# Centring the output projection's weights of two Mamba blocks, so that the normalisation behind it needs no mean

## The chip, the cores and the metric

The kernel runs on one core of a Trainium2 chip. Its engines are TensorE (PE, with its weight loads shown apart as PEld), VectorE (DVE), ScalarE (ACT), GpSimd (POOL) and SyncE (SP, which here issues DMAs). The metric is the device time of one execution in microseconds (us), the median over several executions. The profile is of one execution.

## The reference

A 2 x 256 x 32 x 32 image goes through four layers; the change touches the first one only. It is a GroupNorm and two Mamba blocks, each followed by a layer norm over the 256 channels that is added to the block's input:

```python
def layernorm(x, w, b):
    mu = jnp.mean(x, axis=-1, keepdims=True)
    var = jnp.mean(jnp.square(x - mu), axis=-1, keepdims=True)
    return (x - mu) * jax.lax.rsqrt(var + LN_EPS) * w + b
# mamba_block, per token: project 256 -> 2 x 512, convolve over 4 tokens, silu -> xs
h = dA_t * h + dBu_t                  # 512 channels x 16 states, one step per token
y = einsum(h, C_t) + xs * Dp
y = y * silu(res)
out = y @ out_w + out_b               # 512 -> 256
# the layer
xt = xt + layernorm(mamba_block(xt, m1...), ln1_w, ln1_b)
xt = flip(xt)
xt = xt + layernorm(mamba_block(xt, m2...), ln2_w, ln2_b)
```

The mean that the layer norm takes away is the mean over the 256 outputs of `y @ out_w + out_b`. It is linear in `out_w` and `out_b`: if each of the 512 rows of `out_w`, and `out_b`, has its own mean over the 256 columns taken away, the output has mean zero.

## The kernel before, in words

Layer 0 takes the first 1050 us or so. The 2048 tokens (two images of 1024) are kept as 256 channels on two sets of 128 partitions. Each block handles them in four chunks of 512, so there are eight units, 0 to 7: units 0 to 3 are block m1's, 4 to 7 block m2's. At the heart of a unit is `scan` (L525): 16 states, for each of them four quarters of 128 channels, 64 slots in all. For a state POOL multiplies two products of 128 x 1024 (`m_h`, by way of the helper `lined` at L179, which keeps POOL's work in the order written; residual adds, sums and some DMAs go through the same line). For a slot ACT computes a decay `m_da` of 128 x 512 by Exp (L617) into one of three PSUM buffers, and DVE runs the recurrence over 512 tokens in place on `m_h` (L621). The `m_h` tiles have six buffers, two to a state. PE then transposes each finished `m_h` (L575, L577) into one of three PSUM buffers, and its product with C is added up over the states by DVE (L591) or, for some states, put aside by ACT (L589, `m_ya` and `m_s`) and added by a DMA that POOL issues.

Beside the scan of a unit run the front of the next unit (`front`, L411: convolution on PE, whose result ACT takes out of PSUM at L436 as `m_xs`, then Silu under another table of functions, then the step sizes) and the back of the unit before it (`back`, L650). `back` computes the gate (L655), joins the sums, multiplies by the gate (L689), then projects to 256 outputs per token: for each 128 tokens a product of a row of ones with the bias `out_b` (L696) and four products with the 512 x 256 weights `out_sb` (L700). `norm_rows` (L181) normalises the four tiles of 128 x 256 in the chunk. DVE takes each tile's mean and variance (L188, L189); ACT computes the reciprocal root by Ln and Exp (L159, L160); DVE forms an offset, minus the mean times the root, in two small operations of 128 x 4 (L192, L200); and ACT scales and shifts each tile (L202). PE transposes the result, ACT applies the layer norm's own weight and bias (L724), and POOL adds it to the residual `x`. For the last unit of m2 the same is written into another tile.

`load_rest` (L360) loads the gate's weights and the output weights (L369, a DMA of 512 KB from SP): before the first unit for m1, and at slots 37 and 62 of unit 4 for m2, into the same buffer that m1's held. The two bias rows come in one DMA at the start (L101). At the start, `enter` for unit 0 runs alone: PE projects, ACT takes each of four tiles out (`m_pre`, L405), and the first front follows.

The order is made in two steps. For each unit, `layer0` collects a list `steps` of generators, each with a count, a first and an end slot, and a pacing function advances them between the slots of the scan. That is the order in which instructions are written. A scheduler then orders each engine's instructions by when it reckons their operands to be ready, except where an order is forced (`issue_after`, which `lined` and the table loads use). Each engine then executes in the order so found, and an instruction that waits holds up those behind it on its engine.

Of the kernel before, what the change touches and what calls it, by code (L numbers as in the profile page):

```python
# [10 lines left out]
F32 = mybir.dt.float32  # L11
I32 = mybir.dt.int32
BF16 = mybir.dt.bfloat16
AF = mybir.ActivationFunctionType
# [5 lines left out]
P = 128  # L20
# [4 lines left out]
C = 256  # L25
# [6 lines left out]
NDC = DI // P  # L32
# [37 lines left out]
class Net:  # L70
# [110 lines left out]
    def norm_rows(self, outs, ins, by=None):  # L181


        nc, n = self.nc, len(ins)
        mv = self.small.tile([P, n, 2], F32, tag="ln_mv", name="ln_mv")
        for i, a in enumerate(ins):
            st = self.small.tile([P, 6], F32, tag="ln_st", name="ln_st")
            nc.vector.bn_stats(out=st, in_=a)  # L188
            nc.vector.bn_aggr(out=mv[:, i, :], in_=st)  # L189
        if by is nc.scalar:  # L190
            off = self.small.tile([P, n], F32, tag="ln_off", name="ln_off")
            nc.vector.tensor_sub(off, self.zeros[:, :n], mv[:, :, 0])  # L192
        rs = self.small.tile([P, n], F32, tag="ln_rs", name="ln_rs")
        if by is nc.gpsimd:
            nc.gpsimd.tensor_scalar_add(rs, mv[:, :, 1], self.eps5)
            nc.gpsimd.tensor_tensor(rs, rs, self.power[:, :n], ALU.pow)
        else:
            self.rstd(rs, mv[:, :, 1])
        if by is nc.scalar:
            nc.vector.tensor_mul(off, off, rs)  # L200
            for i, (o, a) in enumerate(zip(outs, ins)):
                nc.scalar.activation(  # L202
                    o, a, AF.Identity, scale=rs[:, i : i + 1], bias=off[:, i : i + 1]
                )
            return
        for i, (o, a) in enumerate(zip(outs, ins)):
            nc.vector.tensor_scalar(o, a, mv[:, i, 0:1], rs[:, i : i + 1], ALU.subtract, ALU.mult)
# [79 lines left out]
class Mamba:  # L287
# [73 lines left out]
    def load_rest(self):  # L361

        net, nc, m, wpool = self.net, self.net.nc, self.m, self.wpool
        in_w, out_w, xproj_w, dt_w = self.weights
        self.gate_sb = wpool.tile([P, NCC, DI], F32, tag="gate_w", name=f"{m}_gate_sb")
        nc.sync.dma_start(self.gate_sb, in_w[:, :, DI:])
        yield
        self.out_sb = wpool.tile([P, NDC, C], F32, tag="out_w", name=f"{m}_out_sb")
        nc.sync.dma_start(self.out_sb, out_w)  # L369

        if self.kept:
            nc.sync.dma_start(self.skip_tile(), self.kept[1])
        else:
            self.scaled(self.skip_tile(), f"{m}_D")
        yield

    @staticmethod
    def first(j):
# [364 lines left out]
def paced(n, parts):  # L743

    taken = [0] * len(parts)
    for slot in range(n):
        for i, (steps, many, first, end) in enumerate(parts):
            while taken[i] < many and slot >= first + (end - first) * taken[i] / many:
                next(steps, None)
                taken[i] += 1  # L750
        yield
    for steps, *_ in parts:
        for _ in steps:
            pass
# [11 lines left out]
def layer0(net, x, x_dram, m1, m2, load_image, taps, conv_dram, lg):  # L766
# [4 lines left out]
    tc, nc = net.tc, net.nc  # L771
    with (
# [45 lines left out]
        for u, (m, j) in enumerate(units):  # L818
            joined = u + 1 < len(units)
            ready = done  # L820
            if joined:
                done = [islice(b, 2 * NDC + 11) for b in done]
            steps = [(b, NDC, 4, 20) for b in done]
            if u:
                m.due.update(units[u - 1][0].due)
            fronts = []
            for a, k in units[u + 1 : u + 2]:
                if k == 0:
                    a.load()
                fronts.append(a.front(k))  # L830
                if u == 0:
                    steps.append((a.enter(k), Mamba.ENTER, 0, 10))
            enters = []
            for a, k in units[u + 2 : u + 3]:
                if k == 0:
                    a.load_in()
                enters.append(a.enter(k))
            steps += [(f, Mamba.HEAD - 3, 0 if u else 10, 25) for f in fronts]
            steps += [(b, NDC + (not joined), 25 if joined else 19, 37 if joined else 35) for b in done]
            steps += [(f, 3, 25, 33) for f in fronts]  # L840
            if u == NCH - 2:

                steps.append((blocks[1].fetch_diagonals(), 1, 34, 35))
            rest = m.load_rest() if u and j == 0 else iter(())
            steps += [(rest, 1, 37, 38)]
            for n, first, end in Mamba.STEPS:
                steps += [(f, n, first, end) for f in fronts]
            steps += [(b, 8, 45, 53) for b in done]
            steps += [(e, Mamba.ENTER - 1, 36, 44) for e in enters]
            steps += [(e, 1, 59, 60) for e in enters]  # L850
            steps += [(b, 2, 1, 5) for b in late]
            steps += [(b, 1, 54, 55) for b in done] + [(b, 2, 56, 58) for b in done]
            if u + 1 == len(units):
                steps += [(b, 2, 60, 63) for b in done]
            late = ready
            steps += [(rest, 1, 62, 63)]
            if u + 1 < len(units):
                more = not u
                for n, first, end in ((2, 12, 32), (4, 35, 47), (3, 58, 63)):
                    steps += [(islice(aside, n + more), n + more, first, end)]  # L860
            else:
                last.close()
                m.ps_da = last.enter_context(tc.tile_pool(name="m_da2", bufs=2, space=PSUM))
                ps_acc = last.enter_context(tc.tile_pool(name="m_acc", bufs=1, space=PSUM))

                def place(u):
                    pool, tag, w = {
                        3: (one, "pre", TC + 3), 0: (two, "xs", TC), 1: (two, "delta", TC),
                        2: (two, "du", TC),
                    }[u]  # L870
                    a = pool.tile(
                        [P, NDC, w], F32, tag=tag, name=f"early_{u}",
                        bufs=3 if tag == "xs" else None,
                    )
                    return taps.load(u, a.rearrange("p d t -> p (d t)"))

                pair = {u: place(u) for u in taps.ORDER}
                def early():
                    for k in range(2):
                        a = ps_acc.tile([P, TC], F32, tag="acc", name=f"early_acc{k}")  # L880
                        acc = {k: taps.bank(a)}
                        yield from taps.convolve(0, pair, acc)
                        taps.read(acc, lg)

                steps += [(early(), 112, 3, 63)]
            own = m.back(j, u + 1 == len(units), u + 2 < len(units))
            if u + 1 == len(units):

                steps += [(islice(own, 5), 5, 44, 58)]
            before = m.scan(j, before, paced(63, steps), u == 0, u + 1 == len(units))  # L890
            done = [own]
# [1249 lines left out]
def conv_attn_hybrid(ctx: ExitStack, tc: tile.TileContext, a: dict, out: bass.AP):  # L2141
# [9 lines left out]
    with tc.tile_pool(name="conv_w", bufs=2) as convw:  # L2151
        def load_x(b):
            for cc in range(NCC):
                nc.sync.dma_start(x[:, cc, b, :], a["x"][b, cc])

        load_x(0)
        taps = Taps(net, convw, main, x, a["l1_w1"], a["l1_w2"])
        layer0(
            net, x, a["x"],
            [a[f"m1_{k}"] for k in ("in_w", "out_w", "xproj_w", "dt_w")],  # L2160
            [a[f"m2_{k}"] for k in ("in_w", "out_w", "xproj_w", "dt_w")],
            lambda: load_x(1), taps, conv_dram, lg,
        )
# [144 lines left out]
```

## Time and profile before

| | |
|---|---|
| median of 6 runs | 2037.71 us (2033.49 to 2049.37) |
| the profiled execution | 2038.84 us, of which the span is 2037.1 us |
| granted PE clock, mean over the span | 0.966 |
| PE, busy | 1865.2 us, 92% of the span |
| PE weight loads, busy | 1339.8 us, 66% |
| DVE, busy | 1334.9 us, 66% |
| POOL, busy | 1071.2 us, 53% |
| ACT, busy | 946.5 us, 46% |
| ACT's scaling pass L202 in layer 0 | 28 + 4 passes, 13.5 + 1.9 us |
| DVE's statistics L188 in layer 0 | 32 passes, 12.3 us |

In a line of instructions the fields are: the start (or, in groups, none), the busy time in us, the engine, the line of the kernel, the operation, output<-inputs by the program's names, shapes and the number of instructions; in square brackets, or after the last bar, the idle time of the engine just before and the instruction that ended it. In groups "12.3, 420" is the busy time of the group in us and the mean duration of one in ns. Where an engine works through a pipeline, successive instructions overlap a little, so the busy time of a group can be smaller than the count times the mean.

### The profile page before, as it was taken

How to read it: one execution, taken by the hardware profiler on the slowest of the kernel's cores; microseconds unless marked ns; L12 is line 12 of the kernel's file. 1: busy time of each engine (PE TensorE's matmuls, PEld its weight loads, DVE VectorE, ACT ScalarE, POOL GpSimd, SP SyncE). 2: the span in 40 equal slices, each digit the busy share in tenths (PEclk: the TensorE clock that was granted, in tenths of full speed). 3: DMA queues.
4: the chain of work that ended last, by engine and by line, in shares of the span. 5: the costliest groups of instructions: out<-in, count | busy, mean ns of one | idle time of the engine just before them, and what ended most of it. 6: DMA issues, size and time to landing. Idle time of an engine off the chain costs nothing. (4 is left out here: it accounts for less than half of the span.)

```text
span 2037.1 us, 27880 instructions
## 1 busy us (share of the span) xinstructions
PE 1865.2 (92%) x9938; PEld 1339.8 (66%) x9938; DVE 1334.9 (66%) x2141; ACT 946.5 (46%) x1713; POOL 1071.2 (53%) x726
## 2 busy tenths in 40 slices
PE   8788988898898988899999989999999899999995
PEld 3465665656565665655666555568999656799994
DVE  6989998999889989897614285774222455652223
ACT  4787777777877767764302253332111122221111
POOL 7888896978979798985404250012333200023330
PEclk9889999999999999899999999999999999999997
DMA  4334354343535334362130100146999400358995
GB/s 151 98 91 120 88 145 112 88 110 85 143 91 134 77 86 112 88 156 47 32 57 1 52 0 1 37 183 250 328 328 335 162 21 21 143 191 319 328 329 196
DMA packets 98856, 271.77 MB, mean 133 GB/s; under 512 B 35915, under 2 KB 54224, under 8 KB 82324
## 3 DMA queue, kind: packets, MB, share of 16 engines
q1 hardware_dynamic: 81268, 198.03, 28.9%
q0 software_dynamic: 14432, 68.31, 13.5%
q10 hardware_dynamic: 3008, 3.55, 0.5%
q8 instruction: 83, 1.36, 0.3%
q14 instruction: 65, 0.53, 0.1%
HBM read 200.80 MB, written 22.77 MB: 110 GB/s over the span
## 5 line engine op out<-in xcount | busy, mean ns | idle before, releaser
L179 POOL TENSOR_TENSOR m_h<-m_du,m_b 128x1024 f32<-128x1024 f32 x254 | 603.8, 2463 | 143.0 <-PE m_ht L577 61.3
L617 ACT ACTIVATE m_da<-m_delta,m_aneg 128x512 f32<-128x512 f32 x512 | 349.4, 694 | 150.7 <-DVE m_h L621 145.2
L621 DVE TENSOR_TENSOR_SCAN m_h<-m_da,m_state,m_h 128x512 f32<-128x512 f32 x256 | 314.3, 1268 | 20.6 <-POOL m_h L179 13.1
L577 PEld LDWEIGHTS m_ht<-ident,m_h 128*128 128x128 f32 x1600 | 193.4, 146 | 191.9 <-DVE m_h L621 64.8
L621 DVE TENSOR_TENSOR_SCAN m_h<-m_da,m_h 128x512 f32<-128x512 f32 x256 | 299.6, 1210 | 18.9 <-ACT m_da L617 13.3
L577 PE MATMUL m_ht<-ident,m_h 128*128 128x128 f32 x1600 | 253.6, 286 | 59.0 <-DVE m_h L621 29.7
L591 DVE SCALAR_TENSOR_TENSOR m_ya<-m_ht,m_ct,m_ya 128x512 f32<-128x512 f32 x324 | 232.6, 737 | 59.9 <-PE m_ht L577 50.9
L2067 PEld LDWEIGHTS h<-xts,we_l_late 128*128 128x128 f32 x2048 | 238.4, 192 | 7.7 <-issue 2.8
L2067 PE MATMUL h<-xts,we_l_late 128*128 128x128 f32 x2048 | 239.7, 275 | 3.3 <-DMA we_l_late<-in_l_experts_dram 1.5
L2075 DVE TENSOR_TENSOR hid<-hid,h 128x512 f32<-128x512 f32 x79 | 54.3, 687 | 232.2 <-PE h L2067 231.8
L1806 POOL DMA_INDIRECT x_l_early<-l_zs,l_source x15 | 17.3, 1156 | 341.6 <-ACT pt L1570 139.5
L2074 ACT ACTIVATE hid<-h 128x512 f32<-128x512 f32 x79 | 47.2, 597 | 314.3 <-PE h L2067 314.3
L575 PE MATMUL m_ht<-ident,m_h 128*128 128x128 f32 x896 | 138.2, 302 | 29.9 <-ACT m_s L589 11.9
L575 PEld LDWEIGHTS m_ht<-ident,m_h 128*128 128x128 f32 x896 | 122.0, 208 | 52.8 <-DVE m_h L621 19.9
L1806 POOL DMA_INDIRECT x_l_late<-l_zd,source x64 | 65.4, 1022 | 147.9 <-PE xt L2050 143.8
L2082 PE MATMUL o<-we_l_late,hid 128*128 128x256 f32 x512 | 122.7, 381 | 4.1 <-DVE y L2087 2.8
L2089 POOL DMA_INDIRECT l_yd<-y,target x64 | 65.4, 1022 | 104.1 <-DVE y L2087 92.0
L430 PE MATMUL m_conv<-m_pre,m_taps 128*128 128x512 f32 x240 | 116.9, 605 | 3.4 <-ACT m_xs L436 3.3
L589 ACT ACTIVATE m_s<-m_ht,m_ct 128x512 f32<-128x512 f32 x156 | 104.5, 687 | 29.6 <-DMA m_yb<-m_s 12.9
L2082 PEld LDWEIGHTS o<-we_l_late,hid 128*128 128x128 f32 x512 | 91.8, 190 | 15.3 <-DVE y L2087 3.9
L1001 PE MATMUL early_acc<-x,early 128*98 128x448 f32 (+24 forms) x308 | 100.3, 452 | 0.4 <-DVE lg L1018 0.4
L1001 PE MATMUL acc<-x,pair 128*98 128x416 f32 (+21 forms) x308 | 93.3, 450 | 0.0
(412 smaller groups left out, 3119.7 us busy)
## 6 DMA issues: line engine op xcount, KB each, us to landing
we_l_late<-in_l_experts_dram SPq DMA_DIRECT2D x64, 1536.0 KB, 9.1
m_yb<-m_s POOLq DMA_DIRECT2D x39, 1024.0 KB, 8.6
m_b<-m_bd SPq DMA_DIRECT2D x128, 256.0 KB, 3.5
we_l_early<-in_l_experts_dram SPq DMA_DIRECT2D x15, 1536.0 KB, 8.1
m_ya<-m_yb POOLq DMA_DIRECT2D x7, 1024.0 KB, 8.8
w<-in_l_w_dram SPq DMA_DIRECT2D x21, 256.0 KB, 6.5
l_yl<-l_yd SPq DMA_DIRECT2D x8, 512.0 KB, 11.1
l_zd<-l_z SPq DMA_DIRECT2D x7, 512.0 KB, 3.0
```

Of the source, the lines that this page charges most:

```text
L179: self.line = do(*args, **named)
L430: nc.tensor.matmul(ps, lhsT=self.taps[:, dc * 4 + k, :], rhs=pre[:, dc, k : k + TC], start=(k == 0), stop=(k == 3),)
L575: nc.tensor.matmul(a, lhsT=h, rhs=net.ident, start=True, stop=True)
L577: nc.tensor.transpose(a, h, net.ident)
L589: nc.scalar.activation(to[:, i, :], ps, AF.Copy, scale=c)
L591: nc.vector.scalar_tensor_tensor(ya[:, i, :], ps, c, ya[:, i, :], ALU.mult, ALU.add)
L617: net.decayed = nc.scalar.activation(da, delta[:, dc, :], AF.Exp, scale=self.aneg[:, i : i + 1])
L621: nc.vector.tensor_tensor_scan(h, da, h, 0.0 if first else state[:, n, dc : dc + 1], ALU.mult, ALU.add)
L1001: nc.tensor.matmul(a[:, lo - 16 * k : hi - 16 * k, co : co + n], lhsT=lhsT, rhs=self.x[:, kc, b, lo - r0 : hi - r0, ci : ci + n], start=(u ...
L1806: nc.gpsimd.indirect_dma_start(out=x, out_offset=None, in_=rows[:, :], in_offset=bass.IndirectOffsetOnAxis(ap=source[:, g : g + 1], axis=0 ...
L2067: nc.tensor.matmul(ps[:, at], lhsT=w12[:, s, kc, at], rhs=xt[:, kc * P : (kc + 1) * P], start=(kc == 0), stop=(kc == NCC - 1),)
L2082: gate.o = nc.tensor.matmul(ps[:, :C], lhsT=ht[:, mc * P : (mc + 1) * P], rhs=w[:, 8 + mc, :], start=(mc == 0), stop=(mc == NHC - 1),)
```

## The change

Once per block, `centre` takes the mean over the columns out of each row of the output weights, and out of the bias. It does it in place with ACT: for each of the four tiles of 128 x 256 and for the bias row, a Copy that also adds up its row (`accum_out`); two small passes that turn sums into minus means; and for each tile and the bias an Identity with that number as its bias. That is 12 instructions a block. They are written for slots 6 to 36 of each block's second unit (`j == 1`), ahead of the first `back` of the block. In `norm_rows`, the two small DVE operations on the offset are gone, and ACT's pass is a Copy with a scale alone, without an offset. The statistics are taken as before; of them, only the variance is used where ACT does the pass.

```diff
         for i, a in enumerate(ins):
             st = self.small.tile([P, 6], F32, tag="ln_st", name="ln_st")
             nc.vector.bn_stats(out=st, in_=a)
             nc.vector.bn_aggr(out=mv[:, i, :], in_=st)
-        if by is nc.scalar:
-            off = self.small.tile([P, n], F32, tag="ln_off", name="ln_off")
-            nc.vector.tensor_sub(off, self.zeros[:, :n], mv[:, :, 0])
         rs = self.small.tile([P, n], F32, tag="ln_rs", name="ln_rs")
...
         if by is nc.scalar:
-            nc.vector.tensor_mul(off, off, rs)
             for i, (o, a) in enumerate(zip(outs, ins)):
-                nc.scalar.activation(
-                    o, a, AF.Identity, scale=rs[:, i : i + 1], bias=off[:, i : i + 1]
-                )
+                nc.scalar.activation(o, a, AF.Copy, scale=rs[:, i : i + 1])
             return
...
+    def centre(self):
+
+        nc, w = self.net.nc, self.out_sb
+        sums = self.wpool.tile([P, NDC + 1], F32, tag="centre", name=f"{self.m}_centre", bufs=1)
+        parts = [(w[:, dc, :], sums[:, dc : dc + 1]) for dc in range(NDC)]
+        parts.append((self.out_b, sums[:1, NDC:]))
+        for a, s in parts:
+            nc.scalar.activation(a, a, AF.Copy, accum_out=s)
+            yield
+        nc.scalar.activation(sums[:, :NDC], sums[:, :NDC], AF.Copy, scale=-1.0 / C)
+        nc.scalar.activation(sums[:1, NDC:], sums[:1, NDC:], AF.Copy, scale=-1.0 / C)
+        for a, s in parts:
+            nc.scalar.activation(a, a, AF.Identity, bias=s)
+            yield
...
             rest = m.load_rest() if u and j == 0 else iter(())
             steps += [(rest, 1, 37, 38)]
+            if j == 1:
+                steps.append((m.centre(), 10, 6, 36))
             for n, first, end in Mamba.STEPS:
```

`NDC` is 4 and `C` is 256.

## The prediction

> **What bounds the kernel now.** I read the stretches of the span first, then the idle time of VectorE (DVE) and ScalarE (ACT) by releaser, then the groups of instructions that the change touches, then the timeline around a block's normalisation. The change lies in layer 0 alone (0 to about 1050 us; eight units of 512 tokens, a scan of 115.6 to 121.8 us each and 139.1 for the last). Busy time by stretch (length, PE, weight loads, DVE, ACT, POOL, clock, DMA share, GB/s), alternately from state 12 of a unit to state 5 of the next, and from there to state 12:
>
> ```profile
> 238.00:305.00 67.00, 59.84 (x315) 42.29 (x316) 62.54 (x71) 52.98 (x96) 66.41 (x33) 0.97 0.44 118
> 305.00:357.00 52.00, 44.88 (x225) 28.38 (x223) 44.18 (x49) 38.74 (x65) 33.64 (x18) 0.93 0.41 110
> 357.00:424.00 67.00, 58.95 (x312) 40.27 (x313) 62.46 (x72) 53.24 (x98) 66.76 (x33) 1.00 0.43 111
> ...
> 592.00:658.00 66.00, 56.96 (x303) 39.18 (x303) 62.85 (x69) 51.78 (x97) 65.76 (x33) 1.00 0.46 117
> ...
> 910.00:1045.00 135.00, 131.69 (x623) 83.55 (x621) 83.75 (x124) 44.33 (x69) 54.11 (x38) 0.99 0.18 41
> ```
>
> In the 67 us stretches POOL is busy 99% and DVE 62.5 us, so DVE has 4.5 us of room; the 52 us stretches have no full engine, there chains of DVE, PE and ACT set the length. The last unit is PE's. Who waits for whom (total us, times, longest):
>
> ```profile
> ACT m_da L617 <- DVE m_h L621: 145.2, 188, 6.8
> ...
> DVE m_ya L591 <- PE m_ht L577: 50.9, 43, 5.0
> ...
> DVE m_h L621 <- ACT m_da L617: 20.5, 24, 3.6
> ...
> DVE m_h L621 <- POOL m_h L179: 17.3, 17, 6.4
> ```
>
> ACT mostly waits for DVE's scans to free one of three decay buffers, so it is at most three scans ahead: an ACT instruction that stalls longer than that lead stops the scan.
>
> **What is removed.** The groups of the edit (busy us, mean ns, idle before and its releaser):
>
> ```profile
> L200 DVE TENSOR_TENSOR ln_off<-ln_off,ln_rs 128x4 f32<-128x4 f32 x8 | 7.2, 896 | 4.3 <-ACT ln_rs L160 4.2
> ...
> L192 DVE TENSOR_TENSOR ln_off<-zeros,ln_mv 128x4 f32<-128x4 f32 x8 | 3.6, 450 | 0.0
> ```
>
> These 16 instructions go: 7.2 + 3.6 + 4.3 = 15.1 us at most; measured as the delay of the next DVE instruction at each block (2.3, 1.0, 2.3, 0.9, 2.3, 2.8, 1.0, 0.4) it is 13.0. The first five (8.8 us) lie inside the stretches where POOL is full. A scan that starts earlier there only waits longer for POOL's product, as these two of DVE already do:
>
> ```profile
> 406.42 5.06 DVE L621 TENSOR_TENSOR_SCAN m_h<-m_da,m_state,m_h 128x512 f32<-128x512 f32 x4 [0.38 <-POOL m_h L179]
> 411.95 3.63 DVE L621 TENSOR_TENSOR_SCAN m_h<-m_da,m_state,m_h 128x512 f32<-128x512 f32 x3 [0.47 <-POOL m_h L179]
> ```
>
>  I count these five as nothing; if POOL's limit did not cover them, they would be worth all of it. The sixth (853 us) lies where POOL runs 8 to 10 us ahead; half of 2.8, **-1.3**. The last two lie in PE's unit, 131.69 busy of 135: **-0.4** of 1.4. ACT's 32 scaling passes drop one pointer operand; by rows of 128x512 with two operands (775 ns) and one (687) that is 32 x 0.09 = 2.8 us of an engine with 14 us free in each stretch: 0, at most -2.8.
>
> **What is added, at the start.** The 24 ACT instructions of `centre` are written for states 1 to 8 of each block's second unit, but in the built kernel's order the first block's stand at the very head of ACT: four sums over the output weights come before the first `m_pre`, and the rest between the four `m_pre`.
>
> ```profile
> 6.42 0.34 SPq L369 DMA_DIRECT2D m_out_sb<-in_m_out_w_dram  x1
> ...
> 13.73 0.69 ACT L405 ACTIVATE m_pre<-m_in,cols_sb 128x512 f32<-128x512 f32 x1 [2.70 <-PE m_in L399]
> 15.45 0.69 ACT L405 ACTIVATE m_pre<-m_in,cols_sb 128x512 f32<-128x512 f32 x1 [1.03 <-PE m_in L399]
> ```
>
> The weights take 7.1 us, so they land at 13.5. A sum over 128x256 is in no row; bounds are 373 ns (copies of that shape, L1100) and 565 (L202, two operands). Four take 1.5 to 2.3, so the first `m_pre` starts at 15.0 to 15.8 instead of 13.73, with the projection's third product, which needs its buffer, behind it. Between the others ACT idles 1.03 us, into which two or three of the remaining passes fit each time. What waits is the first convolution, which ends PE's opening at 26.4: **+1.0** (0 if the slack takes it, 2 if the sums are slow).
>
> **What is moved.** POOL's order is unchanged; PE and DVE follow. ACT's order changes in every block's normalisation and the unit after it. At state 1 of the next unit it was (m_xs is line 436, waiting for POOL's residual add):
>
> ```profile
> 401.89 0.69 ACT L617 ACTIVATE m_da<-m_delta,m_aneg 128x512 f32<-128x512 f32 x1 [0.58 <-DVE m_h L621]
> 404.11 0.69 ACT L436 ACTIVATE m_xs<-m_conv,cols_sb 128x512 f32<-128x512 f32 x1 [1.53 <-POOL x L179]
> 404.70 0.68 ACT L589 ACTIVATE m_ya<-m_ht,m_ct 128x512 f32<-128x512 f32 x1
> ```
>
> Now `m_xs` and the second `m_ya` stand ahead of that last decay of state 1. POOL's add is not earlier, so the decay starts at 404.11 + 2 x 0.6 = 405.3, plus the first `m_ya` if it too is queued behind, 405.9: its scan at 406.6 instead of 404.8, +1.8. Behind it the scans of states 2 to 4 catch up what they waited for POOL (0.4 to 0.5), leaving +1.3; DVE at state 5 then does two `m_ya` before the scan that frees ACT for its block of Silus and table loads. I carry **+1.5** into the next stretch for each of three boundaries (units 1-2, 2-3, 3-4): +4.5. Ends for each: 0, if DVE's 4.5 us of room takes it, and 3.0, if the Silu block slips by DVE's two passes (2 x 0.74) as well. Earlier, around states 14 and 15, the scaling and transposed passes also come ahead of two decays; with a scan waiting 1 us longer there, the same room absorbs it before the later stall, so it isn't added.
>
> Between units 4 and 5 the second block's centring comes in. Its first sum stands behind `m_s` of state 13 and waits for its weights, issued at 612.28 with 5.4 us to land: 617.7, where ACT is free at 616.65. That is 1.0 us, plus 0.4 of work, and behind it queue the second `m_s`, the `ln_rs` and the last decay of state 14. Three more sums stand before state 1's decays, and `m_xs` now ahead of the third decay: +1.5 as above and +1.0 of the wait, **+2.5** (1 to 5). The five subtracting passes (0.5 each, by four L202 in 1.93 us) are spread through states 1 to 5 where ACT idles for DVE: 0; without that cover, 2.5, which is in the upper end. Units 5-6 have `m_xs` ahead of two decays: **+1.5** (0 to 3). Unit 0-1 keeps its order: 0. SyncE's only move, one scan row past one or two loads in five units, has rows prefetched four deep: 0, up to 0.5 each. The table loads stay at 24.
>
> **The sum.** +1.0 + 4.5 + 2.5 + 1.5 - 1.3 - 0.4 = +7.8 us on the profiled execution's 2038.84 (span 2037.1): 2046.6. That execution stands 1.1 above the median of 2037.71, so 2045.5 by the median; I say 2046. Within 0.5% (10.2 us) is about what a measurement of this kernel can tell from no change; its six runs spread over 15.9.
>
> **Two rules.** DVE's 16 removed passes took 99 to 2370 ns against 150 when undisturbed, while POOL's products keep 2.35 us around them. The Trainium skill ("SBUF — State Buffer", section "SBUF: two separate sides") says that a VectorE operation with two SBUF inputs and a GpSimd operation share a port pair as an exclusive lock; by that POOL's full stretches could gain up to 16 x 0.15 = 2.4 us, an estimate, and the sum would be +5.4; no row here shows POOL held. DVE's scaling passes of 128x512 took 578 ns (L282), ACT's 687 (L589). The skill ("ScalarE: Activation LUTs", "Rules for kernel authors") gives add and multiply to VectorE rather than ScalarE, which speaks against centring on ACT: 16 passes of half that width, about 0.9 us of ACT by those two rows.
>
> **Rivals.**
> *The removed chain counts in full.* For: its longest pass, up to 2.4 us, holds DVE just where ACT waits for DVE. Against: POOL's 99%. Then 13.0 + 2.8 come off and only +1.0 and +2.5 stay: -12.3, 2026.5 less 1.1, **2025**.
> *The order of ACT costs double.* One place decides: state 1's last decay behind `m_xs`. If the lateness reaches the Silu block whole, each of five boundaries costs 3.0, with the start at 2.0 and the wait for weights 2.0: +19, **2057**. It decides from about 2.2 us a boundary on. For: no decay can be issued until those passes are through, and no scan without it; against: DVE's room.
> *Room takes everything.* DVE's 4.5 us per POOL stretch swallow the stalls: +1.0 + 1.0 - 1.7 = +0.3, less 1.1: **2038**.
>
> **How the numbers follow.** Forecast 0.42 (its own range 2040 to 2052; 0.28 within 0.5%, that is to 2047.9, and 0.14 above); double 0.28; room 0.12; full gain 0.18. So faster 0.18, within 0.40, slower 0.42. Each outer case leaves about half or a third of itself out (0.18/2, 0.28/3), 0.18 in all: 2026 to 2058.
>
> **What would show it.** After: the first `m_pre` at 15 or later; the decay of state 1 behind `m_xs` with its wait for POOL about as long as before; DVE's scan there waiting for ACT; POOL's stretches still 99%. If DVE's waits for POOL shrink while units don't grow, the room was larger; if units 1 to 3 are shorter than 116, POOL was no limit and I am wrong on the side of the gain.

## The result and the profile after

The changed kernel takes 2048.05 us (median of 22 runs, 2043.67 to 2057.21) against 2039.47 us for the kernel before, run beside it (48 runs, 2032.37 to 2049.37). The ratio is 1.0042, with a 95% interval of 1.0031 to 1.0053: it is slower by 8.6 us, or 0.42%. The forecast was +7.8 us on the profiled execution, and 2046 us in all. The profiled execution of the changed kernel took 2051.44 us, its span 2049.7.

Busy time by stretch in the changed kernel, the stretches set to its own units (same columns as before). The first, third and fourth rows are the stretches in which POOL was full:

```profile
241.00:308.00 67.00, 59.66 (x317) 42.60 (x317) 61.08 (x69) 51.90 (x94) 66.42 (x33) 0.97 0.45 118
308.00:361.00 53.00, 45.65 (x238) 29.86 (x237) 47.27 (x52) 41.50 (x73) 36.29 (x19) 0.97 0.42 110
361.00:426.00 65.00, 57.68 (x301) 39.28 (x300) 58.58 (x66) 50.08 (x92) 64.17 (x32) 0.97 0.44 114
...
595.00:661.00 66.00, 58.28 (x294) 40.07 (x292) 56.71 (x64) 51.64 (x101) 63.51 (x32) 0.95 0.44 112
...
914.00:1049.00 135.00, 131.24 (x633) 84.27 (x631) 83.98 (x121) 44.77 (x72) 56.16 (x42) 1.00 0.19 43
```

POOL still has 99% of the stretch around 241 to 308, but 96% of the one around 595 to 661, where the second block's centring falls: there POOL is no longer the full engine. The last unit is PE's as before.

Who waits for whom in layer 0 of the changed kernel (total us, times, longest):

```profile
ACT m_da L626 <- DVE m_h L630: 149.7, 200, 5.1
...
DVE m_ya L600 <- PE m_ht L586: 52.2, 44, 4.7
...
DVE m_h L630 <- ACT m_da L626: 32.0, 35, 3.6
...
ACT m_xs L445 <- POOL x L179: 14.7, 5, 5.8
...
DVE m_h L630 <- POOL m_h L179: 12.9, 8, 6.4
```

In the kernel before, ACT's wait for the add was:

```profile
ACT m_xs L436 <- POOL x L179: 8.6, 5, 4.2
```

The other lines of before stand in the prediction. DVE's scans waited 20.5 us for ACT's decays and now wait 32.0; they waited 17.3 us for POOL's products and now wait 12.9. ACT waited 8.6 us for POOL's residual add before it could take `m_xs` out, now 14.7. DVE's own work fell by 9.3 us over the whole span (1334.9 to 1325.6), and none of it shows in the time.

The place that the prediction replayed, state 1 of unit 3, on ACT and then on DVE:

```profile
401.59 0.69 ACT L626 ACTIVATE m_da<-m_delta,m_aneg 128x512 f32<-128x512 f32 x1 [1.14 <-DVE m_h L630]
405.68 0.69 ACT L445 ACTIVATE m_xs<-m_conv,cols_sb 128x512 f32<-128x512 f32 x1 [3.40 <-POOL x L179]
406.27 1.26 ACT L598 ACTIVATE m_ya<-m_ht,m_ct 128x512 f32<-128x512 f32 x2
407.41 0.70 ACT L626 ACTIVATE m_da<-m_delta,m_aneg 128x512 f32<-128x512 f32 x1
```

```profile
408.14 1.28 DVE L630 TENSOR_TENSOR_SCAN m_h<-m_da,m_state,m_h 128x512 f32<-128x512 f32 x1 [1.69 <-ACT m_da L626]
409.98 7.16 DVE L630 TENSOR_TENSOR_SCAN m_h<-m_da,m_state,m_h 128x512 f32<-128x512 f32 x6 [0.55 <-ACT m_da L626]
```

ACT stands idle for 3.4 us at `m_xs` because POOL's add is no earlier than it was, both `m_ya` go first, and the decay that the scan needs starts at 407.41. In this execution the unit began 1.6 us later than before (395.4 against 393.9). The scan that started at 404.8 before starts at 408.14, so 1.8 us of it is new, as the prediction had it. DVE then waits for ACT where it waited for POOL before.

**A table of stages.** Layer 0 can be split at the starts of DVE's scans: the first scan; then, added up over the eight units, states 0 to 6, states 7 to 12 and states 13 to 15. Each row is one profiled execution; the runs e1 to l4 are described below. Times are in us.

| execution | first scan | states 0-6 | states 7-12 | states 13-15 | last scan ends |
|---|---|---|---|---|---|
| before | 44.1 | 385.1 | 381.4 | 196.7 | 1007.3 |
| before, again (e8) | 44.1 | 385.1 | 382.3 | 197.2 | 1008.8 |
| before, layer 0 alone (l1) | 45.9 | 384.9 | 378.1 | 195.8 | 1004.8 |
| before, new addresses (e2) | 45.1 | 385.0 | 382.4 | 197.2 | 1009.7 |
| changed | 45.6 | 393.8 | 374.8 | 195.9 | 1010.2 |
| changed, layer 0 alone (l2) | 45.2 | 393.1 | 379.3 | 196.5 | 1014.0 |
| changed, old addresses (e1) | 45.5 | 389.1 | 376.6 | 198.9 | 1010.1 |
| normalisation alone (e3) | 45.3 | 391.9 | 382.1 | 198.1 | 1017.3 |
| centring alone (e4) | 45.2 | 386.2 | 382.8 | 198.5 | 1012.6 |
| centring late (e5) | 44.1 | 395.1 | 374.3 | 195.2 | 1008.7 |
| centring late, layer 0 alone (l3) | 43.9 | 397.1 | 381.7 | 193.7 | 1016.4 |
| decays first (e6) | 44.1 | 390.1 | 378.0 | 192.3 | 1004.5 |
| decays first, layer 0 alone (l4) | 45.4 | 391.6 | 375.2 | 193.6 | 1005.8 |
| before, one slot later (e7) | 45.4 | 387.5 | 378.6 | 198.2 | 1009.7 |

In four executions with the order of before, states 0 to 6 take 384.9 to 385.1 us. In the three with the changed order (changed, l2, e1) they take 389.1, 393.1 and 393.8: all are longer, but by 4 to 9 us, so the column tells the two orders apart and doesn't give the price of the change to the microsecond. The same holds for e5 and l3 and for e6 and l4, two executions each of one order in layer 0: 2.0 and 1.5 us apart. Units 3 and 4 do repeat: in the changed order their states 0 to 6 are 1.1 and 2.0 to 2.1 us longer in all three, in e3, e5 and l3 too. Units 5 and 6 do not, and there PE's granted clock differs as well. States 1 and 2 of unit 5 took 12.9 us in the changed kernel at a clock of 0.87, and 10.6 in l2 and e1 at 1.00. Over states 0 to 6 of unit 6 the clock was 0.93 and 0.94 in the changed kernel and l2, and 0.97 in e1 and before. Whether the changed order brings these dips on is open.

States 7 to 12 differ by 4 us between executions of the order of before, so one profile can't tell anything of that size there. The changed kernel's own profile had 374.8 us there and ended layer 0 only 2.9 us late, although 8.8 us had been lost in states 0 to 6. From the first scan to the end of the last, the four executions of before take 958.8 to 964.7 us and the three of the changed order 964.6, 964.6 and 968.8: on the mean 3 us more.

### The profile page after: what moved, and what is told of

Its sections match the earlier page's. It is cut to its first block, busy times and chain, and to the rows that moved or that the text cites. A ratio compares the mean times of both kernels' runs of the same rounds, so it can differ in the third digit from the quotient of the medians.

```text
span 2049.7 us, 27896 instructions
## 1 busy us (share of the span) xinstructions
PE 1868.3 (91%) x9938; PEld 1342.3 (65%) x9938; DVE 1325.6 (65%) x2125; ACT 952.3 (46%) x1747; POOL 1071.0 (52%) x726
## 3 DMA queue, kind: packets, MB, share of 16 engines
q0 software_dynamic: 14432, 68.31, 13.5%
## 5 line engine op out<-in xcount | busy, mean ns | idle before, releaser
L630 DVE TENSOR_TENSOR_SCAN m_h<-m_da,m_state,m_h 128x512 f32<-128x512 f32 x256 | 314.3, 1268 | 23.2 <-POOL m_h L179 12.1
L2078 PE MATMUL h<-xts,we_l_late 128*128 128x128 f32 x2048 | 244.1, 278 | 7.2 <-DMA we_l_late<-in_l_experts_dram 3.7
L2078 PEld LDWEIGHTS h<-xts,we_l_late 128*128 128x128 f32 x2048 | 242.5, 195 | 12.2 <-issue 7.4
L584 PEld LDWEIGHTS m_ht<-ident,m_h 128*128 128x128 f32 x896 | 120.8, 206 | 48.1 <-ACT m_s L598 14.7
```

The lines of the kernel that those rows point to most:

```text
L584: nc.tensor.matmul(a, lhsT=h, rhs=net.ident, start=True, stop=True)
L630: nc.vector.tensor_tensor_scan(h, da, h, 0.0 if first else state[:, n, dc : dc + 1], ALU.mult, ALU.add)
L2078: nc.tensor.matmul(ps[:, at], lhsT=w12[:, s, kc, at], rhs=xt[:, kc * P : (kc + 1) * P], start=(kc == 0), stop=(kc == NCC - 1),)
```

## The experiments

The comparisons below are of the whole kernel unless layer 0 is named, each with the ratio to the kernel before on the same chip.

**e1 and e2: is it the addresses?** The dropped offsets freed 128 bytes per partition in a pool that lies under most tiles, and the sums took 32 back, so most tiles moved by 128 or 96 bytes. e1 is the changed kernel with the sums in the room of the offsets, e2 the kernel before with the offsets in the room of the sums:

```diff
# e1, on the changed kernel
-        sums = self.wpool.tile([P, NDC + 1], F32, tag="centre", name=..., bufs=1)
+        sums = self.net.small.tile([P, NDC + 1], F32, tag="ln_off", name=...)
# e2, on the kernel before (net.offs is the pool m_w)
-            off = self.small.tile([P, n], F32, tag="ln_off", name="ln_off")
+            off = self.offs.tile([P, n], F32, tag="centre", name="ln_off", bufs=1)
```

> The changed kernel with its order of instructions, but the column sums take the room of the dropped offsets, so that every other tile lies at the address it had before the change (in the changed kernel most tiles lie 128 or 96 bytes lower). The profile of the change shows layer 0 ending only 2.9 us later than before, while the medians differ by 8.6. Address theory: the other 5.7 come from the lower addresses; then this run is about +3 us over the kernel before (2042 to 2043) and layer 0 ends +3. Order theory: addresses are nothing, the whole +8.6 stays (2048), and the profiled executions merely differ in the later layers.

> The kernel before, with its order of instructions, but its tiles at the addresses of the changed kernel: the offsets are kept in a tile of 32 bytes where the sums would be. Address theory: +5 to +6 us, nearly all in the later layers. Order theory: no change, within 2 us, layer 0 ending within 0.5 us of before.

e1 measured 1.0021 (1.0006 to 1.0037), 2045.48 us; e2 1.0023 (1.0006 to 1.0040), 2045.95 us. Taken alone they look like an effect of the addresses of 0.2%, about 4 us. Both lie nearer to what the address theory expected (about +3, and +5 to +6) than to the order theory's +8.6 and 0, and the two together (0.21% and 0.23%) make up the changed kernel's 0.42%. The profiles fit that in part: from the end of the last scan to the end of the span, the two executions at the new addresses (changed, e2) took 1039.5 and 1038.8 us, and the eight whole-kernel ones at the old addresses 1029.3 to 1037.0. Against it stands e3 (below), which loses 8.8 us at the old addresses. In layer 0, e2's states 0 to 6 and 13 to 15 are those of before to 0.5 us, so what the addresses cost would arise elsewhere. In e1, states 0 to 6 cost 4.0 us, less than in the changed kernel. Whether the addresses cost nothing or up to about half of the 8.6 us is open.

**e3 and e4: which half of the change costs?** e3 has only the changed normalisation, e4 only the centring in front of the old one; both with tiles at the addresses of before.

```diff
# e3, on the changed kernel: no centring; ACT's Ln writes to the room of the offsets
-            if j == 1:
-                steps.append((m.centre(), 10, 6, 36))
# e4, on the kernel before: centre() added, norm_rows untouched
+            if j == 1:
+                steps.append((m.centre(), 10, 6, 36))
```

> The changed normalisation alone (no offsets, one operand less in ACT's pass), on weights that are not centred, with no centring instructions; tiles at the addresses of before. It leaves out the centring, so the mean is not removed from the output. ACT's and DVE's order is that of the changed kernel in all but the centring's own instructions, so this carries the moved m_xs at state 1. Order theory: layer 0 pays at the boundaries but not at the start: units 3, 4, 5, 6 each show their state 1 longer by 1 to 2 us, layer 0 ends 0 to +3, total 0 to +6. Rival (the removed chain counts in full): -10 to -12 us. Rival (room takes everything): 0 within 1.

> The centring alone, in front of the normalisation as it was before (offsets kept); tiles at the addresses of before; ACT's order is that of before apart from the centring's instructions. Order theory: +1.5 us at the start, where the profile of the change shows the first scan at 45.6 instead of 44.1, and +1 to +2 between units 4 and 5 from the wait for the weights: +2.5 to +3.5 in layer 0 and in total. If the centring carries the whole loss: +8.

e3 measured 1.0043 (1.0024 to 1.0062), 2048.74 us; e4 1.0005 (0.9984 to 1.0026), 2043.38 us against 2042.34. So taking sixteen instructions off DVE costs as much by itself as the whole change, more than expected, and adding 24 to ACT costs little, less than expected in the total. In the table e3 pays 6.9 us in states 0 to 6. Its first scan is late without any centring, as in other runs that have none (last section). e4 pays 1.1 to 1.2 in states 0 to 6, of which 1.1 lie in state 6 of unit 0, ahead of every boundary, where the granted clock was 0.87 over 13.5 us and 1.00 in the kernel before. The expected +1 to +2 between units 4 and 5 shows as 0.4, in unit 5. The order of e3's instructions on ACT is the changed kernel's but for some in units 4 and 5, that of e4 is that of before but for a few in unit 5. The rival in which the removed chain counts in full wanted -10 to -12 for e3: it falls.

The start in the kernel before, and in e4, whose granted clock was 1.00 there as well (PE: start, busy; in brackets the idle time and its releaser):

```profile
11.71 7.13 PE L399 MATMUL m_in<-x,m_in_sb 128*128 128x512 f32 x16 [0.44 <-DVE x L282]
```

```profile
11.82 3.70 PE L414 MATMUL m_in<-x,m_in_sb 128*128 128x512 f32 x8 [0.44 <-DVE x L282]
15.98 3.70 PE L414 MATMUL m_in<-x,m_in_sb 128*128 128x512 f32 x8 [0.46 <-ACT m_pre L420]
```

PE's projection, one unbroken row of 7.13 us before, now breaks after its second product and waits for `m_pre`, as the prediction said. The first scan is 1.1 us later in e4, 1.4 in e1; the prediction had 1.0.

**e5: the centring held back.** Each of its instructions may follow only the decay written just before it, so that the start is as it was, and the second block's sums come after the weights have landed.

```diff
# on e1
+            with tc.issue_after(net.decayed.ins):
                 nc.scalar.activation(a, a, AF.Copy, accum_out=s)
...
+            with tc.issue_after(net.decayed.ins):
                 nc.scalar.activation(a, a, AF.Identity, bias=s)
```

> Both parts of the change, tiles at the addresses of before, but each instruction of the centring may only follow the decay written just before it. So ACT issues none at the start, and the second block's sums come in states 1 to 4 of unit 5, long after its weights have landed. The rest of the order stays that of the changed kernel. Order theory: against the run with both parts at the old addresses (+4.3 us) the start's 1.4 us and the wait of about 1 us for the weights go: +1 to +3 over before, first scan at 44.1 to 45, DVE's waits for ACT's decays still 28 us or more. If the centring were the loss, it would fall to 0 or below.

It measured 1.0059 (1.0041 to 1.0077): 12 us slower than before, a clear miss. The start did return (44.1), but states 0 to 6 went to 395.1, 10 us over before. Of this, 1.5 lie in unit 1 and 2.3 in unit 5, where the centring now is (unit 5 has 1.0 in e1, without it); 1.2 lie in unit 0, where the clock was 0.87 as in e4; and 5.2 lie in units 3, 4, 6 and 7, as in the changed order. The 1.5 us in unit 1 are in all four executions with the centring held back (49.7 to 49.8 against 48.2 in the other ten), so ACT's idle time beside the scan is not free. That an instruction fixed between two decays makes the next decay late is the likely way, not shown: DVE's waits for decays in unit 1 rise from 1.1 us to 2.0 in e5, 3.4 in e6 and 3.3 in l4, but l3 has 0.8. These sums don't account for all that e5 loses beyond e1, 0.38% or 8 us.

**e6 and e7: the decays first.** In e6, on e5, the normalisation and the two steps behind it are written one slot of the scan later; e7 does only this to the kernel before.

```diff
-            steps += [(b, 1, 54, 55) for b in done] + [(b, 2, 56, 58) for b in done]
+            steps += [(b, 1, 55, 56) for b in done] + [(b, 2, 57, 59) for b in done]
```

> As the run before (both parts, old addresses, centring held back), and the normalisation of a chunk and the two steps behind it are written one slot of the scan later. By this ACT's scaling passes stand behind the decays of state 15 instead of ahead of them, and at the next unit's state 1 m_xs stands behind the last decay, as in the kernel before. Order theory: DVE's waits for ACT's decays fall from 29 us back to about 20, and the loss goes: -3 to +1 us against before. Rival (room takes the stalls, so the order is nothing): as the run before, +1 to +3. Rival (the removed chain counts in full once the order is right): -9 or lower.

> The kernel before with only that shift of the normalisation by one slot, offsets kept, no centring: the control for the run before it. Theory: -1 to +2 us; what the removal of the offsets is worth with the decays first is the difference between that run and this one: 0 to -3 us if POOL covers it, -9 or more if the chain counts in full.

e6 measured 1.0016 (0.9998 to 1.0033), 2041.62 us, and e7 1.0022 (1.0003 to 1.0042), 2044.74 us. One slot takes 9 us off e5. ACT in e6 at state 1 of unit 3:

```profile
403.80 0.69 ACT L629 ACTIVATE m_da<-m_delta,m_aneg 128x512 f32<-128x512 f32 x1 [0.58 <-DVE m_h L633]
406.01 0.69 ACT L448 ACTIVATE m_xs<-m_conv,cols_sb 128x512 f32<-128x512 f32 x1 [1.51 <-POOL x L179]
```

The decay is ahead of `m_xs` again, as it was before the change. DVE's waits for ACT did not fall to 20 us as expected: they are fewer, 24 in place of 34, but for 29.2 us in place of 30.3. Against the kernel before, 4.9 us more of them lie in units 1 and 5, where the centring is, and 5.8 more in units 3 and 4, where none is. So what the shift mends is not the sum of these waits. Both runs came out above what was expected: e6 at +3.3 us (-3 to +1 expected) and e7 at +4.5 (-1 to +2), so that the shift by itself costs in the kernel before. What the removal of the offsets is worth with the decays first is e6 against e7: 0.0006 of 2038.6 us, 1.2 us, with intervals that leave room for a gain of 6 and a loss of 4; in e6 it also has to pay for the centring held back. In states 0 to 6 e7 pays 2.5 us for the shift alone, e6 5.0. A gain of 9 or more is not there.

**e8: the kernel before, again.**

> The kernel before, unchanged, as if it were a variant: what two samples of one kernel differ by, and how far one profiled execution differs from another, stage by stage. If the profiled executions differ by several us in the later layers and in the states 10 to 14 of the units, then neither the 5.7 us of the later layers nor single units may be read from one profile: expected within 2 us in the medians, within 1 us at the end of the first scan, within 3 us at the end of layer 0, within 6 us at the end.

It measured 1.0003 (0.9988 to 1.0018). The profiled executions of the one kernel differ by 1.5 us at the end of layer 0 and 2.1 at the end, with single states up to 2.5 us apart. So the median of one kernel is good to about 0.15%. The later layers of a single profile, about 9 us longer in the changed kernel's and in e2's, 7 in e5's and none in e4's, are weak evidence for a cause there.

**l1 to l4: layer 0 alone.** To see where the 8.6 us arise, the later layers were left out, in four kernels on one chip:

```diff
# after layer0(...), in place of the later layers
+    for b in range(NB):
+        for cc in range(NCC):
+            nc.sync.dma_start(out[b, cc], x[:, cc, b, :])
```

> Layer 0 of the kernel before alone: the later layers are left out and x, as layer 0 leaves it, is written out instead. The order of instructions in layer 0 and the addresses are those of the whole kernel. It is the base for the three runs that follow: by the profile about 1045 us of work and 10 to 15 us for the output, 1055 to 1065, and executions that lie closer together than the whole kernel's 16 us.

> Layer 0 of the changed kernel alone, in the same way. Theory on record (all of the loss is the order of ACT and the start): +7.8 us over layer 0 of before. Reading of the single profiles (layer 0 ended 1.4 to 2.9 us later): +1 to +3, and the other 5 to 7 us of the whole kernel's +8.6 arise in the later layers.

> Layer 0 alone, both parts of the change at the old addresses, centring held back until the second unit of a block. Order theory: 1.1 to 1.4 us faster than layer 0 of the changed kernel, for the start, less what 12 instructions of ACT cost in units 1 and 5 where DVE waits for ACT. If instead this run's +12 us of the whole kernel arise in layer 0, it is 3 us slower.

> Layer 0 alone, as the run before with the normalisation written one slot later (decays first, m_xs behind the decay). Order theory: 3 to 5 us faster than the run before, at or below layer 0 of the kernel before. If the order of ACT at the boundaries costs nothing: within 1 us of the run before.

| layer 0 alone (5 runs each) | median us | lowest and highest | ratio to the whole kernel before |
|---|---|---|---|
| before (l1) | 1047.84 | 1046.14 to 1053.81 | 0.5148 (0.5130 to 0.5167) |
| changed (l2) | 1056.45 | 1052.71 to 1057.17 | 0.5173 (0.5160 to 0.5186) |
| centring late (l3) | 1059.35 | 1054.86 to 1061.18 | 0.5186 (0.5171 to 0.5201) |
| decays first (l4) | 1049.61 | 1049.18 to 1051.78 | 0.5148 (0.5137 to 0.5160) |

By the medians layer 0 loses 8.6 us, by the ratios 0.0025 of 2038.5, 5.1 us, with overlapping intervals, because l1 had two runs near 1053. Five runs of each leave room for a loss of 1 to 10 us. So layer 0 loses time, as the theory on record had it; whether it carries all of the whole kernel's 8.6 or only a part isn't settled by these runs. The base itself was missed: l1 was expected at 1055 to 1065 us. The order of the four is that of the whole kernels: late is worst, decays first stands at the base. l3 was expected to be faster than l2 and is slower, as e5 was. The one slot of e6 is worth 9.7 us here by the medians, 7.7 by the ratios (3 to 5 expected).

ACT's wait for the add, in the layer 0 of before, of the changed kernel and with the decays first, each from its answer on waits:

```profile
ACT m_xs L436 <- POOL x L179: 8.9, 5, 4.2
```

```profile
ACT m_xs L445 <- POOL x L179: 13.9, 5, 6.8
```

```profile
ACT m_xs L448 <- POOL x L179: 4.9, 4, 1.6
```

No version here beats the kernel before. One that was not run would have the decays first and the centring at the start, but behind the last `m_pre`; what it would take is open.

## Why the prediction was right, point by point

**The bound.** Right in kind: the stall is one of order, at the decay of state 1, and it takes the place of a wait for POOL. The loss in units 3 and 4 repeats in every execution with the changed normalisation at the old slot. In the table it is part of the 4.0 to 8.8 us that states 0 to 6 lose. e3 shows that the order costs without the centring, and e6 that moving the normalisation by one slot returns 9 us.

**The removed instructions.** Right in kind for the first five blocks: no gain is seen, and e3 shows that it is not the centring that eats one. ACT's scaling passes became shorter as estimated, from 15.4 us to 12.5 in all. The sixth and the last two did better or as forecast. These are DVE's small operations in unit 6 before the change, and DVE in the same place after it:

```profile
853.23 1.68 DVE L192 TENSOR_TENSOR ln_off<-zeros,ln_mv 128x4 f32<-128x4 f32 x1
...
855.97 1.25 DVE L200 TENSOR_TENSOR ln_off<-ln_off,ln_rs 128x4 f32<-128x4 f32 x1
```

```profile
860.24 3.45 DVE L630 TENSOR_TENSOR_SCAN m_h<-m_da,m_h 128x512 f32<-128x512 f32 x3
```

Three scans now run on end. States 13 to 15 of unit 6 fall from between 21.9 and 23.2 us to 20.4, so by 1.5 to 2.8 where 1.3 was taken; the last unit's fall by 0.3 (0.4 taken). But unit 7's states 0 to 6 are 0.5 to 0.9 longer, which was not foreseen and gives part of it back.

**The start.** +1.0 forecast, +1.1 and +1.4 in e4 and e1, where it can be read by itself. The first `m_pre` of the changed kernel began at 15.45 us, inside the stated 15.0 to 15.8. The price of a sum lay inside its bounds: one takes two instructions, which overlap so that the next sum starts 0.40 us later.

```profile
L378 ACT ACTIVATE m_out_sb<-m_out_sb 128x256 f32<-128x256 f32 x8 | 3.2, 406 | 3.5 <-DMA m_out_sb<-in_m_out_w_dram 3.5
...
L378 ACT ACTIVATION_READ_ACCUMULATOR m_out_sb<-m_out_sb 128x1 f32 x8 | 1.5, 187 | 0.0
```

**The boundaries.** The terms were not right, and their sum was so in only two of three executions. States 0 to 6 of the unit behind each boundary, against the mean of the four executions of before, in us:

| boundary | taken | changed | l2 | e1 |
|---|---|---|---|---|
| units 1-2 | +1.5 | 0 | -0.1 | -0.2 |
| units 2-3 | +1.5 | +1.1 | +1.1 | +1.1 |
| units 3-4 | +1.5 | +2.0 | +2.1 | +2.1 |
| units 4-5 | +2.5 | +3.9 | +1.7 | +1.0 |
| units 5-6 | +1.5 | +1.2 | +2.4 | -0.5 |
| sum of the five | +8.5 | +8.2 | +7.2 | +3.5 |
| units 6-7 | 0 | +0.7 | +0.9 | +0.5 |

The weak step is to price one boundary by a replay and to carry the same +1.5 to the others. At units 1-2 POOL's add stood closer to the decays: `m_xs` there waited 0.56 us, not 3.40, and the decay behind it was not late enough to hold a scan. DVE ran six scans on end there:

```profile
288.12 0.69 ACT L445 ACTIVATE m_xs<-m_conv,cols_sb 128x512 f32<-128x512 f32 x1 [0.56 <-POOL x L179]
...
289.28 1.30 ACT L626 ACTIVATE m_da<-m_delta,m_aneg 128x512 f32<-128x512 f32 x2
```

```profile
288.41 6.89 DVE L630 TENSOR_TENSOR_SCAN m_h<-m_da,m_h 128x512 f32<-128x512 f32 x6
```

The wait for the second block's weights was as forecast, 1.0 us; it lies in unit 4, ahead of the states of this table. The second line is `m_xs` in state 1 of unit 5, which waits for POOL:

```profile
619.97 0.42 ACT L378 ACTIVATE m_out_sb<-m_out_sb 128x256 f32<-128x256 f32 x1 [0.98 <-DMA m_out_sb<-in_m_out_w_dram]
...
640.53 0.69 ACT L445 ACTIVATE m_xs<-m_conv,cols_sb 128x512 f32<-128x512 f32 x1 [2.40 <-POOL x L179]
```

**The part that was put at nothing.** That the scaling passes now come ahead of decays 15 was said to vanish in DVE's room. In the changed kernel, l2 and e1, states 13 to 15 are 0.8 to 1.3 us longer in units 1 and 3 and 1.0 to 2.8 in unit 4 (the wait for the weights included), and between 2.0 shorter and 0.2 longer in unit 5. With the decays put first (e6, l4) these states fall to 192.3 and 193.6 from the 195.9 to 198.9 of the changed order. The same slot with the offsets kept leaves them at 198.2 (e7), so the fall needs the removal too. So this term was not zero; in the sum over the units, what unit 6 gained hid it.

**The rivals.** Full gain: refuted by e3. Room takes everything: refuted, DVE's room of 4.5 us took none of the stalls before state 7. Behind it, in states 7 to 12, the three executions with the changed order (changed, l2, e1) lie at 374.8 to 379.3 us and the four with that of before at 378.1 to 382.4, 4 us apart on the mean, so that some recovery there is possible; the scatter hides it. Double cost: not reached; it needed 2.2 us a boundary on the mean of five, and the measured mean is 1.6 in the changed kernel, 1.4 in l2 and 0.7 in e1. The Trainium skill's lock on the ports that VectorE and GpSimd share ("SBUF — State Buffer", section "SBUF: two separate sides") would have given POOL an estimated 2.4 us back. Nothing of the kind shows, but the loss from the order lies over it, so no run here decides it.

**The number.** That +8.6 comes so near to +7.8 is in part luck. In e1, at the old addresses and with a clock in units 5 and 6 no lower than before, the boundaries give 3.5 us of the 8.5 taken, and the whole kernel lost 4.3 (1.2 to 7.6). The changed kernel's profile reaches 8.2 with a lower clock there, gives 6.6 back in states 7 to 12, and is about 9 us longer in the later layers, for which the prediction had no term. So it is shown that the changed order of ACT costs time, and where; how much of the 8.6 us it makes up beside the clock and the addresses is open.

## What to carry to other kernels

Where a scheduler orders instructions by when it reckons their operands ready, removing a few short operations may move long ones: compare the orders on each engine before adding up durations, and look for an instruction that waits for a slow engine and has come ahead of one that the critical engine needs. Idle time of an engine that runs a fixed distance ahead of another need not be free room: work pinned into it cost 1.5 us in unit 1 (e5). And check on several executions, of both kernels, which stages repeat; here states 0 to 6 repeat to 0.2 us in the kernel before, but only to 5 in the changed order, and states 7 to 12 only to 4 or 5 in either.

## What was not expected of the hardware

Executions of the same order differ in PE's granted clock at particular places, and this is as large as what was to be measured. In state 10 of unit 2 the kernel before had, from 345 to 351 us, a granted clock of 0.65 in one profile and 0.81 in the next (the third column from the end; first the kernel before, then e8):

```profile
345.00:351.00 6.00, 6.00 (x24) 4.03 (x23) 4.00 (x6) 3.85 (x8) 4.56 (x2) 0.65 0.46 103
```

```profile
345.00:351.00 6.00, 6.00 (x26) 4.00 (x26) 4.98 (x7) 4.79 (x10) 4.35 (x2) 0.81 0.60 131
```

That state took 12.0 us in the one and 10.3 in the other. At the start, the products that keep PE busy before the first projection took 0.69 us in the kernel before and 1.20 in e7 (four each), whose start has the same instructions. The granted clock reads 1.00 over the first 18 us in both, so what made them longer is not shown:

```profile
8.77 0.69 PE L246 MATMUL warm<-ident 128*128 128x128 f32 x4
```

```profile
9.22 1.20 PE L246 MATMUL warm<-ident 128*128 128x128 f32 x4
```

e7's first scan began at 45.4 us in place of 44.1, without any centring; e2 and e3 show the same. In l1, which has the order of before, the first scan began at 45.9: there the projection took 8.83 us in place of 7.13, with a granted clock of 0.71 from 10 to 14 us, and the changed kernel's own profile has 8.83 at 0.73. So of the changed kernel's +1.5 at the start one profile alone could not have told the part of the centring.
